# One attention block row computed by symmetry, one convolution on TensorE, and a rewritten schedule in an attention + Mamba kernel

## The chip, the cores and the metric

The kernel runs on one core of a Trainium2 chip, as one launch. The metric is the device time of one execution in microseconds (us). Time before: a median of 10092.66 us in 4 runs (10086.53 to 10095.38).

A core has five engines that run their own instruction streams side by side: PE (TensorE, matrix products; its weight loads are listed as PEld), DVE (VectorE), ACT (ScalarE), POOL (GpSimd) and SP (SyncE, which here only issues DMAs, in order). Semaphores order them.

## The reference

Eight images of 256 channels and 48 x 48 pixels go through two residual layers. Everything is float32.

```
x = x + top16_attention(group_norm(x))     # layer 0
x = x + mamba_depth_2(group_norm(x))       # layer 1

# layer 0, an image of n = 2304 tokens
feat, pos = split(tokens @ W.T + bias)     # 256 columns each
pos = pos / max(norm(pos), 1e-12)
sim = pos @ pos.T                          # 2304 x 2304
out = softmax(top16(sim)) @ feat[top16 tokens]

# layer 1, twice (d = 0, 1): 512 inner channels, 16 states
xi, z = split(layer_norm(x) @ in_w.T)
xc = silu(cb + sum_{k<4} xi[t - 3 + k] * cw[:, k])
dt_r, Bm, Cm = split(xc @ xp_w.T)          # 16 columns each
dt = softplus(dt_r @ dtp_w.T + dtp_b);  A = -exp(A_log)
h[t] = h[t-1] * exp(dt[t] A) + dt[t] Bm[t] xc[t]       # per channel and state
y = (sum_states(h * Cm) + xc * D) * silu(z)
x = y @ out_w.T
```

## The kernel before

**Layer 0** (the generator `layer0`). An image's 2304 tokens are 6 chunks of T = 384 for the statistics and projections (`project`, `features`, `norms`, `inverse_norm`, `scale`) and 18 blocks of 128 rows for the attention. `inverse_norm` starts a reciprocal root on ScalarE (L161) and finishes it with five small instructions of a Newton step on GpSimd (L168 to L172). For a block `t`, `similar` (L391) multiplies the block's positions with all 2304 positions, in five pieces of up to 512 columns and two halves of the 256 channels; `keep_similar` (L400) copies them from PSUM. `top` and `others` (L407 to L414) find the 16 largest on VectorE with two MAX8 and two MATCH_REPLACE8 over 2304 columns. What was replaced marks the chosen ones: ScalarE builds `rest` (L429), TensorE transposes similarities and subtracts a large number where nothing was chosen (`turn`, L437 and L438, tile `pt`), ScalarE exponentiates (`weights`, L446), TensorE multiplies with the features (`weigh`, L457), and the result is turned back and added to x (L464 to L487). The table `within` gives each of these pieces a place, in steps of a block that are 16 apart.

**Layer 1.** The work is cut into 96 units: 8 images x 6 chunks of 384 tokens x 2 depths. A unit has 16 steps, each for 32 inner channels; a step's tile holds 128 partitions (4 groups of states x 32 channels) and 4 states x 385 columns in its free direction. Each step is scanned in two halves. So a unit has 32 *hooks*, the whole program 3072, and the loop at the end of the file writes the order out by hand, hook by hook (manual schedule; the order in the program is the order on each engine). At hook m:

1. `carry` for the half scanned before: if its product was VectorE's, ScalarE copies the last state (`h_st`, L847) and then two zeros (L848) into the columns where the next scan restarts;
2. `decay` for the next half: two ACTIVATE exp of 384 columns into one of two PSUM banks (L815);
3. in the first half of a step: GpSimd makes the input `bx` of the step after next (`make_bx`, L791, from a ring of 8 tiles), multiplies the states of the step before with C where that is its job (`pool_part`, L860), and ScalarE or GpSimd writes the starting states (`take_up`, L805 or L803); in the second half ScalarE copies the last states that GpSimd's part leaves (`carry_pool`, L870);
4. the rows of the table `between` that fall on this hook;
5. `run_scan` (L830): a scan over 770 columns on VectorE; the restart between two sequences is a zero in the decay's first column. Where the letter in `SHARE` is "V", VectorE also multiplies with C (L832); where it is "G", `pool_part` does;
6. the rows of the table `behind`;
7. one piece of the next image's layer 0 (two until its blocks are in step with the hooks).

`SHARE` has a string of 16 letters for units 1 to 9 of an image (12 G), one for units 0, 10 and 11 (8 G) and one for the last image (8 G). The tables place a unit's own steps from 42 hooks before its first scan to 40 behind: layer norm (`mean` to `normal`), `load_in`/`in_proj` (L591), the convolution (`tap`, one ACTIVATE with the last weight, L683; `taps`, three SCALAR_TENSOR_TENSOR per 128 channels on VectorE, L691), `silu_x` (two table loads around four ACTIVATEs, L697 to L700), `x_proj`, `split` (L714, dbl<-px), `step_size`, `softplus`, `times_x` (L741), the loads of `dtr` and `dtxr` for each step (`load_rep`, rings of 3) and of B and C (`load_bc`), then `sum_states` (tile `y`: one matmul with the diagonal of D, L875, and 16 with `sel`, L878, which read the `bx` tiles of four steps), `gate`, `out_proj` and `leave`.

The first image's layer 0 has nothing to lie beside; it runs alone ahead of all this and is ordered by the framework. The projections of the next image's layer 0 all fall into unit 0 of an image, its 18 blocks into the units after. The last image has no layer 0 beside it. Between the two parts, diagonal matrices of D are made (L532), stored to HBM and loaded back one by one as `dmat`.

Of the kernel before, what the change touches and what calls it, by code (L numbers as in the profile page):

```python
# [8 lines left out]
F32 = mybir.dt.float32  # L9
BF16 = mybir.dt.bfloat16  # L10
AF = mybir.ActivationFunctionType
# [7 lines left out]
TINY = 1e-24  # L19
FAR = 64.0  # L20
# [3 lines left out]
def tile_conv_preact(  # L24
# [46 lines left out]
    SHARE = ("GGVGGGVVGGGGGGVG", "GGGVGVVGVVVGVGVG", "VGVGVGVVGGVVGGVG")  # L71
    JR = 1
# [80 lines left out]
    nc.vector.tensor_scalar(A_sb, A_sb, -1.0, None, ALU.mult)  # L153
# [74 lines left out]
    def layer0(b, left, pool, ps0, alone):  # L228
# [50 lines left out]
        def inverse_norm(c):  # L279
            rn[c] = small.tile([P, TB], F32, tag="rn", name=f"rn_{b}_{c}")  # L280
            rsqrt_start(rn[c], n2[c], tiny[:, 1:2])
            rsqrt_end(nc.gpsimd, rn[c], n2[c], TINY, f"rn_{b}_{c}")

# [11 lines left out]
        def chunk(c, xn):  # L295
# [57 lines left out]
            step(lambda: features(0), feature(0))  # L353
            yield
            if c > 0:
                scale(c - 1)
                yield
            for j in range(1, TB):
                step(lambda: features(j), feature(j))
                yield  # L360
            step(norms, norm)
# [9 lines left out]
        leave_psum()  # L371
        yield
        inverse_norm(NCH - 1)
# [11 lines left out]

        def similar(t, i):

            c0, w = widths[i]
            pm = blocks[t]["psim", i] = mm0(w, f"psim_{b}_{t}_{i}")
            for k in range(CB):  # L390
                nc.tensor.matmul(  # L391
                    pm, pos[:, k, t * P : (t + 1) * P], pos[:, k, c0 : c0 + w],
                    start=(k == 0), stop=(k == CB - 1),
                )
# [83 lines left out]
        def finish(t):  # L478
# [14 lines left out]
            (21, weights, 3), (4, top, 3), (14, turn, 0), (15, weights, 0), (6, others, 3),  # L493
            (-5, similar, 4), (-8, keep_similar, 0), (-5, keep_similar, 2), (24, turn_back), (18, weigh, 1),
            (17, weigh, 0), (1, top, 1), (-9, similar, 0), (-8, similar, 1), (-7, similar, 2),
            (22, average), (-6, similar, 3), (-7, keep_similar, 1), (-3, keep_similar, 3), (0, top, 0),
            (-3, keep_similar, 4), (15, turn, 1), (10, others, 4), (5, others, 0), (3, top, 2),
            (6, add_top), (11, invert), (5, others, 2), (17, turn, 2), (20, turn, 3),
            (15, weights, 1), (18, turn, 4), (18, weights, 2), (21, weigh, 3), (7, others, 1),
            (19, weigh, 2), (20, weights, 4), (21, weigh, 4), (24, finish),  # L500
        ]
        begin = min(part for part, *_ in within)
# [12 lines left out]

    lefts = [{} for _ in range(B)]
    with tc.tile_pool(name="first", bufs=1) as pool0, tc.tile_pool(
        name="first_ps", bufs=1, space=PSUM
    ) as ps0:
        for _ in layer0(0, lefts[0], pool0, ps0, True):  # L520
            pass

    diag = hbm.tile([P, DEPTH, DC + 1, DB, P], F32, tag="diag", name="diag", bufs=1)
    with tc.tile_pool(name="setup", bufs=2) as setup:
        for d in range(DEPTH):
            for t in range(DC, DC + 1):
                dg = setup.tile([P, DB, P], F32, tag="dg", name=f"dg_{d}_{t}")
                for k in range(DB):  # L530
                    f = cw[:, d, k, t : t + 1] if t < DC else dpar[:, d, k : k + 1]
                    nc.vector.tensor_scalar(dg[:, k], ident, f, None, ALU.mult)  # L532
                nc.sync.dma_start(diag[:, d, t], dg)
# [6 lines left out]

    banks = [ps.tile([P, 1024], F32, tag=f"da{i}", name=f"da_{i}", bufs=1) for i in range(2)]
    for bank in banks:
        nc.vector.memset(bank, 0.0)

    zeros = const.tile([P, HQ], F32, tag="zeros", name="zeros")
    nc.gpsimd.memset(zeros, 0.0)
# [12 lines left out]
    def load_rep(unit, what, ik):  # L559

        k, i0 = divmod(ik * JR, J)
        t = keep.tile([P, JR, T], F32, tag=f"{what}r", name=f"{what}r_{unit['u']}_{ik}", bufs=3)
        src = unit[f"{what}_d"][k].rearrange("(i g) t -> g i t", g=G)
        for j in range(J):
            nc.sync.dma_start(t[j * G : (j + 1) * G], src[:, i0 : i0 + JR, :])  # L565
        unit[f"{what}r"][ik] = t
# [29 lines left out]
    def load_v(unit):  # L596
        b, c = unit["b"], unit["c"]
        src = unit["left"]["x1"] if unit["d"] == 0 else unit["left"]["v1"][c]
        v = keep.tile([P, CB, T], F32, tag="v", name=f"v_{unit['u']}", bufs=1)
        if unit["d"] == 0:  # L600
            src = src[:, c * T : (c + 1) * T]
        nc.sync.dma_start(v, src.rearrange("(k p) t -> p k t", p=P))
        unit["v"] = v
# [75 lines left out]

    def tap(unit, e):  # L680
        d = unit["d"]
        o = keep.tile([P, T], F32, tag="xc", name=f"xc_{unit['u']}_{e}", bufs=7)
        nc.scalar.activation(  # L683
            o, unit["pe"][e][:, H:], AF.Identity,
            bias=cbias[:, d, e : e + 1], scale=cw[:, d, e, H : H + 1],
        )
        unit["xc"][e] = o

    def taps(unit, e):
        for k in range(H):  # L690
            nc.vector.scalar_tensor_tensor(  # L691
                unit["xc"][e], unit["pe"][e][:, k : k + T], cw[:, unit["d"], e, k : k + 1],
                unit["xc"][e], ALU.mult, ALU.add,
            )
# [77 lines left out]
    ]  # L772
    NSTEP = len(units) * STEPS
# [10 lines left out]
    def make_bx(n):  # L784


        if n >= NSTEP:
            return
        unit, i, k = at(n)
        bx = keep.tile([P, Q, 1 + T], F32, tag="bx", name=f"bx_{n}", bufs=8)  # L790
        nc.gpsimd.tensor_tensor(  # L791
            bx[:, :, 1:], unit["BC"][0],
            unit["dtxr"][i // JR][:, i % JR : i % JR + 1, :].to_broadcast([P, Q, T]), ALU.mult,
        )
        unit["bx"][i] = bx
# [11 lines left out]
    def decay(m):  # L807
# [6 lines left out]
        for s in range(HQ):  # L814
            nc.scalar.activation(  # L815
                da[:, s * (1 + T) + 1 : (s + 1) * (1 + T)], unit["dtr"][i // JR][:, i % JR, :],
# [20 lines left out]
    def carry(m):  # L837


# [4 lines left out]
        if not on_pool(unit, i, p):  # L844
# [3 lines left out]
            nc.scalar.copy(h[:, :, 0], zeros)  # L848
# [52 lines left out]
    def leave(unit, cb):  # L901
# [17 lines left out]
        (-35, center), (7, in_proj, 5), (24, sum_states, 2), (-33, variance), (-21, in_proj, 0),  # L919
        (-15, taps, 1), (38, out_proj, 0), (-15, taps, 2), (-14, taps, 3), (-34, square),  # L920
        (39, leave, 0), (23, load_rep, "dt", 14), (5, load_rep, "dt", 5), (-4, load_bc, 1), (38, out_proj, 1),
        (17, load_d, 2), (-17, tap, 1), (18, load_rep, "dtx", 13), (-8, times_x, 1), (19, gate, 1),
        (-22, normal), (1, load_rep, "dt", 3), (0, load_rep, "dtx", 4), (15, load_rep, "dt", 10), (6, load_rep, "dtx", 7),
        (10, load_rep, "dtx", 9), (12, load_rep, "dtx", 10), (20, load_rep, "dtx", 14), (11, gate, 0), (-29, spread_root),
        (-19, load_in, 5), (33, load_out), (-22, load_in, 0), (21, load_rep, "dt", 13), (-20, tap, 0),
        (-10, step_size, 1), (9, copy_z, 2), (-18, in_proj, 2), (2, load_rep, "dtx", 5), (10, sum_states, 0),
        (13, load_rep, "dt", 9), (29, gate, 2), (9, silu_z), (7, load_rep, "dt", 6), (19, load_rep, "dt", 12),
        (-6, load_rep, "dtx", 1), (-14, load_in, 7), (-30, root), (9, load_rep, "dt", 7), (4, load_d, 1),
        (-24, load_in, 3), (17, load_rep, "dt", 11), (14, load_rep, "dtx", 11), (-13, x_proj), (-17, load_in, 6),
        (-3, load_d, 0), (4, load_rep, "dtx", 6), (-4, load_rep, "dtx", 2), (-42, load_v),  # L930
    ]
    behind = [
        (-12, split), (-3, load_rep, "dt", 1), (3, in_proj, 4), (-10, step_size, 0), (-5, load_rep, "dt", 0),
        (-8, load_rep, "dtx", 0), (-15, tap, 3), (-1, load_rep, "dt", 2), (-28, scale), (16, load_rep, "dtx", 12),
        (11, load_rep, "dt", 8), (8, in_proj, 6), (17, sum_states, 1), (-14, silu_x), (25, load_rep, "dt", 15),
        (-37, affine), (1, times_x, 2), (7, copy_z, 0), (8, load_rep, "dtx", 8), (-17, tap, 2),
        (-10, softplus), (-16, in_proj, 3), (3, load_rep, "dt", 4), (-29, load_in, 2), (6, in_proj, 7),
        (35, gate, 3), (-2, load_rep, "dtx", 3), (8, copy_z, 1), (40, leave, 1), (-3, times_x, 3),
        (22, load_rep, "dtx", 15), (-16, load_in, 4), (29, load_d, 3), (-37, mean), (-19, taps, 0),
        (-19, in_proj, 1), (-10, load_bc, 0), (33, sum_states, 3), (-30, root_end), (-9, times_x, 0),  # L940
        (-22, load_in, 1),
# [90 lines left out]
```

## Time and profile before

| | us |
|---|---|
| median of 4 runs | 10092.66 |
| profiled execution | 10094.78 |
| its span | 10093.1 |
| image 0's layer 0: projections / blocks | 0 to 78 / 78 to 444 |
| unit 0 of image 0 | 501 to 645 |
| unit 0 / units 1 to 9 / units 10 and 11 of image 6 | 7794 to 7933 / to 8822.7 / to 9009 |
| the last image | 9009 to 10080 |

The mean granted clock of TensorE was 0.882 over the span. The span is the time from the first to the last instruction in the trace. "Busy" counts the time in which an engine executes; a group is all instructions of one line, operation and shape; behind the bar stand its busy time and the mean time of one in ns, and behind the second bar the time that the engine stood idle just before such instructions, with what ended most of it. `X <- Y` in a view of waits means that X waited and Y let it go.

### The profile page before, as it was taken

Reading aid. Unit: us, or ns where it says so; the run is one execution under the profiler, and the core shown is the slowest. Engines: PE = TensorE matmul, PEld = TensorE weight load, DVE = VectorE, ACT = ScalarE, POOL = GpSimd, SP = SyncE. Lnnn points to the kernel's source line nnn. Section 1 sums busy time; section 2 is a strip of 40 time slices with the busy share of each in tenths; the row PEclk is TensorE's granted clock in tenths of the full one; section 3 lists DMA queues with packets and bytes.
Section 4 is the critical chain, followed back from the end, with each engine's and each line's share of the span. In section 5 each row is a group of like instructions: output and inputs, shape, how many; then the busy total and the mean of one; then the engine's idle time right before and its main releaser. Section 6 shows DMA issues by size and latency. Waiting matters only on the chain. (4 is left out here: it accounts for less than half of the span.)

```text
span 10093.1 us, 134837 instructions
## 1 busy us (share of the span) xinstructions
PE 8015.8 (79%) x36736; PEld 4390.8 (44%) x36736; DVE 8971.1 (89%) x7992; ACT 7488.2 (74%) x16998; POOL 8943.9 (89%) x3928
## 2 busy tenths in 40 slices
PE   8878886888868888688877888778886888865655
PEld 6544443444534444344443444344443444422222
DVE  4479998899979999799997999989998899988898
ACT  4477786778767777678776777777876778777776
POOL 0079998899989999799997999989998899999998
PEclk9989997899978999799988999889997999977777
DMA  1144444444444444444444444444444444444444
GB/s 31 35 126 122 137 129 143 118 134 125 138 131 130 124 137 129 133 125 137 124 139 126 129 129 135 131 131 127 133 129 145 119 129 128 137 133 133 141 137 121
DMA packets 1243512, 1271.44 MB, mean 126 GB/s; under 512 B 266592, under 2 KB 1215840, under 8 KB 1242752
## 3 DMA queue, kind: packets, MB, share of 16 engines
q1 hardware_dynamic: 1230496, 1262.45, 43.6%
q8 instruction: 293, 4.80, 0.2%
q14 instruction: 467, 3.83, 0.1%
q10 hardware_dynamic: 12256, 0.36, 0.1%
HBM read 1048.94 MB, written 212.86 MB: 125 GB/s over the span
## 5 line engine op out<-in xcount | busy, mean ns | idle before, releaser
L791 POOL TENSOR_TENSOR bx<-BC,dtxr 128x1536 f32<-128x1536 f32 x1536 | 5303.3, 3456 | 87.0 <-PE y L878 42.1
L815 ACT ACTIVATE da<-dtr,A_sb 128x384 f32<-128x384 f32 x6144 | 3586.0, 584 | 814.3 <-DVE bx L830 619.6
L830 DVE TENSOR_TENSOR_SCAN bx<-da,bx 128x770 f32<-128x770 f32 x2040 | 3525.9, 1748 | 191.9 <-ACT da L815 143.3
L860 POOL TENSOR_TENSOR bx<-bx,BC 128x1536 f32<-128x1536 f32 (+1 forms) x1320 | 3307.5, 2506 | 256.6 <-DVE bx L830 239.7
L830 DVE TENSOR_TENSOR_SCAN da<-da,bx 128x770 f32<-128x770 f32 x1032 | 1811.0, 1755 | 247.2 <-ACT da L815 158.2
L591 PE MATMUL pe<-vn,inw 128*128 128x384 f32 (+1 forms) x3072 | 1244.0, 539 | 412.5 <-DVE xr L913 93.2
L391 PE MATMUL psim<-pos 128*128 128x512 f32 (+1 forms) x2880 | 1380.7, 612 | 205.2 <-ACT sim L400 91.7
L457 PE MATMUL po<-feat,aT 128*128 128x256 f32 x5184 | 1360.1, 411 | 20.5 <-ACT aT L446 14.3
L878 PE MATMUL y<-bx,sel 128*32 128x384 f32 x12288 | 1228.7, 536 | 40.2 <-POOL bx L860 30.3
L457 PEld LDWEIGHTS po<-feat,aT 128*128 128x128 f32 x5184 | 1028.3, 205 | 366.6 <-issue 112.7
L832 DVE TENSOR_TENSOR bx<-da,BC 128x768 f32<-128x768 f32 x1032 | 989.3, 959 | 35.5
L591 PEld LDWEIGHTS pe<-vn,inw 128*128 128x128 f32 x3072 | 584.7, 205 | 928.6 <-issue 206.9
L391 PEld LDWEIGHTS psim<-pos 128*128 128x128 f32 x2880 | 553.8, 206 | 840.3 <-issue 466.2
L878 PEld LDWEIGHTS y<-bx,sel 128*32 128x32 f32 x12288 | 397.8, 119 | 860.4 <-issue 736.0
L691 DVE SCALAR_TENSOR_TENSOR xc<-pe,cw,xc 128x384 f32<-128x384 f32 x1152 | 696.5, 612 | 38.4 <-ACT xc L683 11.4
L721 PE MATMUL pd<-dbl,dtp_sb 16*128 16x384 f32 x768 | 416.4, 656 | 342.6 <-ACT dt L730 182.4
L437 PE MATMUL pt<-ident,sim 128*128 128x128 f32 x2592 | 535.8, 289 | 41.9 <-ACT vo L909 18.0
L847 ACT COPY h_st<-da 128x2 f32<-128x2 f32 x832 | 131.6, 158 | 588.5 <-DVE bx L832 581.4
L446 ACT ACTIVATE aT<-pt 128x512 f32<-128x512 f32 (+1 forms) x720 | 387.7, 548 | 233.4 <-PE pt L438 228.8
L896 PE MATMUL pw<-z,ow 128*128 128x384 f32 x1536 | 527.4, 496 | 20.4 <-DVE v L655 7.4
L875 PE MATMUL y<-xc,dmat 128*128 128x384 f32 x768 | 392.7, 598 | 151.4 <-DVE xc L691 125.4
L429 ACT ACTIVATE rest<-left,three 128x512 bf16<-128x512 f32 (+1 forms) x720 | 467.0, 670 | 60.0 <-DVE left L414 60.0
(148 smaller groups left out, 10068.0 us busy)
## 6 DMA issues: line engine op xcount, KB each, us to landing
dtxr<-dtx_d SPq DMA_DIRECT2D x6144, 48.0 KB, 1.8
dtr<-dt_d SPq DMA_DIRECT2D x6144, 48.0 KB, 1.8
BC<-bc_d SPq DMA_DIRECT2D x768, 192.0 KB, 3.7
inw<-in_in_wT_dram SPq DMA_DIRECT2D x768, 128.0 KB, 2.3
dtx_d<-dtx SPq DMA_DIRECT2D x384, 192.0 KB, 2.0
dt_d<-dt SPq DMA_DIRECT2D x384, 192.0 KB, 2.1
ow<-in_out_wT_dram SPq DMA_DIRECT2D x96, 512.0 KB, 4.0
dmat<-diag SPq DMA_DIRECT2D x384, 64.0 KB, 2.1
```

The lines of the kernel that those rows point to most:

```text
L391: nc.tensor.matmul(pm, pos[:, k, t * P : (t + 1) * P], pos[:, k, c0 : c0 + w], start=(k == 0), stop=(k == CB - 1),)
L437: nc.tensor.transpose(pt[:, q], row["sim"][:, r], ident)
L457: nc.tensor.matmul(row["po"], aT[:, m % PT, :], feat[:, m, :], start=(m == 0), stop=(m == NB - 1))
L591: nc.tensor.matmul(pe, w[:, k], unit["vn"][:, k, lo:], start=(k == 0), stop=(k == CB - 1))
L691: nc.vector.scalar_tensor_tensor(unit["xc"][e], unit["pe"][e][:, k : k + T], cw[:, unit["d"], e, k : k + 1], unit["xc"][e], ALU.mult, ALU.add,
L791: nc.gpsimd.tensor_tensor(bx[:, :, 1:], unit["BC"][0], unit["dtxr"][i // JR][:, i % JR : i % JR + 1, :].to_broadcast([P, Q, T]), ALU.mult,)
L815: nc.scalar.activation(da[:, s * (1 + T) + 1 : (s + 1) * (1 + T)], unit["dtr"][i // JR][:, i % JR, :], AF.Exp, scale=A_sb[:, unit["d"], i, ...
L830: nc.vector.tensor_tensor_scan(h, da, g, 0.0, ALU.mult, ALU.add)
L832: nc.vector.tensor_tensor(bx[:, :, 0:T], da.rearrange("p (q t) -> p q t", q=HQ)[:, :, 1:], unit["BC"][1][:, qs], ALU.mult,)
L860: nc.gpsimd.tensor_tensor(g[:, :, 0:T], g[:, :, 1:], unit["BC"][1][:, qs], ALU.mult)
L878: nc.tensor.matmul(y[j * G : (j + 1) * G, :], sel, unit["bx"][k * J + j][:, q, 0:T], start=False, stop=True, skip_group_check=True,)
L896: nc.tensor.matmul(pw, unit["ow"][:, k, cb * P : (cb + 1) * P], unit["z"][k], start=(k == 0), stop=(k == DB - 1),)
```

## The change

1. **Symmetric similarities, in the attention that runs alone.** Each block row of `sim` is stored to HBM from its diagonal on (`store_similar`), and for a later block the sub-blocks left of its diagonal are loaded back (`load_similar`, rows of 512 bytes) and transposed on TensorE. 153 of the 324 sub-blocks of 128 x 128 are made in this way.
2. **Diagonals.** `make_diagonals` makes those of the four convolution weights beside those of D, in both depths, as piece 40 of image 0's layer 0.
3. **TensorE convolution in the last image.** `tap` copies the projected channels to SBUF, `taps` multiplies four shifted windows of them with diagonal matrices on TensorE, and the new `conv_out` adds the bias on ScalarE. The diagonals of both depths are loaded once (2 MB), with the last image's first `load_v`, into tiles that the attention has left.
4. **Restart zeros by the decays.** The `dtr` tile has one more column, set to 1e30 once, so the decay's exp writes the zero itself (385 columns); `carry` copies no zeros, the banks need no memset.
5. **Newton steps.** `inverse_norm` is split: its second half, on GpSimd, comes a piece later, after the first `features` of the next chunk; `scale` a piece after that.
6. **SHARE and the tables** are written anew: 12 G in units 1 to 9 and 8 in the last image as before, at other hooks; 9 instead of 8 in units 0, 10 and 11. Among the rows of `between` and `behind`, `sum_states` 0 moves behind the scan of hook 10 and `sum_states` 1 from behind hook 17 to behind hook 18; many loads and steps move by a few hooks. `within` is also new.

```diff
-    SHARE = ("GGVGGGVVGGGGGGVG", "GGGVGVVGVVVGVGVG", "VGVGVGVVGGVVGGVG")
+    SHARE = ("GGVGGGVVGGGVGGGG", "GGGVGVVGGGVVGVVG", "GVVVGGGVVVGGGVGV")
...
-    nc.vector.tensor_scalar(A_sb, A_sb, -1.0, None, ALU.mult)
+    nc.vector.tensor_scalar(A_sb, A_sb, LEAST, -1.0, ALU.max, ALU.mult)
...
+        def inverse_norm_end(c):
             rsqrt_end(nc.gpsimd, rn[c], n2[c], TINY, f"rn_{b}_{c}")
...
             if c > 0:
                 inverse_norm(c - 1)
-            step(lambda: features(0), feature(0))
-            yield
-            if c > 0:
-                scale(c - 1)
-                yield
-            for j in range(1, TB):
+            for j in range(TB):
                 step(lambda: features(j), feature(j))
                 yield
+                if c > 0 and j == 0:
+                    inverse_norm_end(c - 1)
+                if c > 0 and j == 1:
+                    scale(c - 1)
+                    yield
...
+        def load_similar(t, i):
+            m0, m1 = i * PT, min((i + 1) * PT, t if alone else 0)
+            if m0 < m1:
...
+                nc.sync.dma_start(old[:, 0 : m1 - m0, :], kept[:, m0:m1, t * P : (t + 1) * P])
+                blocks[t]["old", i] = old
+
+        def store_similar(t):
+            if alone and t + 1 < NB:
+                nc.sync.dma_start(kept[:, t, (t + 1) * P :], blocks[t]["sim"][:, (t + 1) * P :])
...
-            for k in range(CB):
-                nc.tensor.matmul(
-                    pm, pos[:, k, t * P : (t + 1) * P], pos[:, k, c0 : c0 + w],
...
+            for m in range(i * PT, min((i + 1) * PT, t if alone else 0)):
+                nc.tensor.transpose(pm[:, m % PT * P : (m % PT + 1) * P], old[:, m % PT, :], ident)
+            lo = max(c0, t * P if alone else 0)
+            if lo < c0 + w:
+                for k in range(CB):
+                    nc.tensor.matmul(
+                        pm[:, lo - c0 :], pos[:, k, t * P : (t + 1) * P], pos[:, k, lo : c0 + w],
...
+    steps = [keep.tile([P, 1 + T], F32, tag=f"dtr{i}", name=f"dtr_{i}", bufs=1) for i in range(3)]
+    for t in steps:
+        nc.vector.memset(t[:, 0:1], NEVER)
...
+            for e in range(DEPTH):
+                nc.sync.dma_start(late["diag"][:, e], diag[:, e, 0:DC])
...
     def tap(unit, e):
         d = unit["d"]
+        if late and unit["b"] + 1 == B:
+            nc.scalar.copy(late["xi"][:, e], unit["pe"][e])
+            return
...
     def taps(unit, e):
+        if late and unit["b"] + 1 == B:
+            cv = unit["cv"][e] = mm(T, f"cv_{unit['u']}_{e}")
+            for k in range(DC):
+                nc.tensor.matmul(
+                    cv, late["diag"][:, unit["d"], k, e], late["xi"][:, e, k : k + T],
...
+    def conv_out(unit, e):
+        if e in unit["cv"]:
...
+            nc.scalar.activation(
+                o, unit["cv"][e], AF.Identity, bias=cbias[:, unit["d"], e : e + 1]
...
-                da[:, s * (1 + T) + 1 : (s + 1) * (1 + T)], unit["dtr"][i // JR][:, i % JR, :],
+                da[:, s * (1 + T) : (s + 1) * (1 + T)], unit["dtr"][i],
...
-            nc.scalar.copy(h[:, :, 0], zeros)
...
-        (9, copy_z, 2), (-18, in_proj, 2), (2, load_rep, "dtx", 5), (10, sum_states, 0),
-        (8, in_proj, 6), (17, sum_states, 1), (-14, silu_x),
+        (18, sum_states, 1), (-19, in_proj, 1), (-18, conv_out, 0), (-14, conv_out, 2), (-14, conv_out, 3),
+        (-14, silu_x), (-39, affine), (5, times_x, 2), (-10, softplus), (-5, load_rep, "dt", 0),
+        (6, in_proj, 7), (10, sum_states, 0), (-10, times_x, 0), (-17, tap, 1), (19, load_rep, "dt", 12),
```

## The prediction

> **What bounds the kernel now.** The page gives busy shares and the dearest groups first. The profiled execution took 10094.8 us, its span 10093.1 us; the median of the runs is 2.1 us lower. The sum below starts from 10094.8 and the 2.1 us come off at its end.
>
> ```profile
> PE 8015.8 (79%) x36736; PEld 4390.8 (44%) x36736; DVE 8971.1 (89%) x7992; ACT 7488.2 (74%) x16998; POOL 8943.9 (89%) x3928
> L791 POOL TENSOR_TENSOR bx<-BC,dtxr 128x1536 f32<-128x1536 f32 x1536 | 5303.3, 3456 | 87.0 <-PE y L878 42.1
> L860 POOL TENSOR_TENSOR bx<-bx,BC 128x1536 f32<-128x1536 f32 (+1 forms) x1320 | 3307.5, 2506 | 256.6 <-DVE bx L830 239.7
> ```
>
> VectorE and GpSimd tie at 89%, but averages hide stages, so I cut the span with the windows view (start:end and length; then PE, PEld, DVE, ACT, POOL busy; granted clock; DMA share; GB/s): the attention that runs alone, unit 0 of image 6, its units 2 to 9, and the last image.
>
> ```profile
> 78.00:444.00 366.00, 354.93 (x1694) 245.19 (x1692) 208.45 (x200) 160.30 (x324) 0.00 (x0) 0.99 0.04 13
> 7794.00:7933.00 139.00, 105.99 (x467) 63.17 (x467) 93.18 (x91) 93.08 (x217) 89.76 (x89) 0.83 0.44 130
> 8029.70:8822.70 793.00, 689.92 (x3273) 386.04 (x3273) 758.68 (x671) 628.68 (x1414) 771.55 (x290) 0.93 0.46 130
> 9009.00:10080.00 1071.00, 635.27 (x2607) 269.83 (x2611) 961.95 (x823) 761.36 (x1797) 997.64 (x411) 0.76 0.47 134
> ```
>
> Each stage has another limit. Alone, TensorE is busy 97%. Unit 0 (seven times) fills no engine. Units 1 to 9 (63 of the 96) are full on GpSimd (97%) and nearly on VectorE (96%). In the last image GpSimd has 93%, VectorE 90%, TensorE 59%.
>
> **1. Symmetric similarities, 366 us alone.** The rows of that window, and the block period from the timeline (start, duration, operation, idle before):
>
> ```profile
> L391 PE MATMUL psim<-pos 128*128 128x512 f32 (+1 forms) x360 | 149.9, 558 | 0.0
> L437 PE MATMUL pt<-ident,sim 128*128 128x128 f32 x324 | 64.0, 281 | 0.0
> ```
> ```profile
> 198.88 2.56 DVE L407 MAX8 top<-sim 128x8 f32<-128x2304 f32 x1 [5.42 <-ACT sim L400]
> ...
> 206.80 2.54 DVE L414 MATCH_REPLACE8 left<-top,left 128x2304 f32<-128x2304 f32 x1
> ...
> 218.63 2.56 DVE L407 MAX8 top<-sim 128x8 f32<-128x2304 f32 x1 [5.42 <-ACT sim L400]
> ```
>
> 149.9 us / 324 sub-blocks of 128 columns = 0.46 us each. A transpose costs at most 64.0/324 = 0.20 us (the rows overlap; four transposes with their four minus products run in 0.68 us, so I take 0.11). 153 of 324 sub-blocks (0+1+...+17) change: 0.26 to 0.35 us each, about −50 us if TensorE alone set the pace. It doesn't: a block takes 19.75 us, of which the selection on VectorE holds 10.4; the next selection starts 9.4 us later, after ScalarE's rest, the attention product, and 6 us of similarities with their copies. With those gone ScalarE's own copies still need about 6 us, so a block stays above about 16.2 us. Only what is cut after the attention product counts, at most some ten sub-blocks a block: 0.33 × (1+2+...+10+3×10) = 0.33 × 85 = **−28 us**, bounds −50 and −15. The store of each finished row block and the load of the old ones (about 1.1 MB a block together) have some 13 us, and DMA stands at 4% there.
>
> **2. Diagonals earlier.** Their eight products (1.53 us), two memsets (0.91 each) and two stores leave the gap between 447 and 452 us; forty products of about 0.2 us go to the first 40 us, where VectorE is 15% busy. **−3 us**; if the x loads queued behind their ten stores on SP were late, +5.
>
> **3. TensorE convolution, last image.** Rows of the last window:
>
> ```profile
> L791 POOL TENSOR_TENSOR bx<-BC,dtxr 128x1536 f32<-128x1536 f32 x190 | 653.4, 3446 | 9.3 <-PE y L878 7.0 <-issue 2.3
> L860 POOL TENSOR_TENSOR bx<-bx,BC 128x768 f32<-128x768 f32 x144 | 314.2, 2182 | 47.5 <-DVE bx L830 46.9
> L691 DVE SCALAR_TENSOR_TENSOR xc<-pe,cw,xc 128x384 f32<-128x384 f32 x132 | 79.9, 612 | 3.1
> L848 ACT COPY da<-zeros 128x2 f32<-128x2 f32 x192 | 31.3, 163 | 40.6 <-DVE bx L832 35.5
> ```
>
> Twelve taps × 0.612 = 7.3 us leave VectorE in each of 12 units. TensorE gets 16 matmuls 384 wide, 0.9 us each by the projection rows of this window (two records, 163.2 us / 184): +14 us on 53 of 90, free as a sum. ScalarE gets four copies of 0.47 (the row dbl<-px) and four outputs of 0.58 (the decay's 0.585) for four taps of 0.66: +1.6 us. GpSimd loses nothing, and its idle time in the whole window is 73 us, 47 of it for scans. So the gain cannot pass 73; 12 × 7.3 = 88 is out of reach. I take half of the scan wait, **−25 us**, bounds −65 and +20. The loss end: conv_out 2 and 3 wait at hook −14 for eight matmuls (7 us, 12 at a low clock) with silu_x and the next decays behind them on ScalarE, and VectorE's scans wait for those. What silu_x itself holds the timeline shows:
>
> ```profile
> 9516.29 1.28 ACT L697 ACT_TABLE_LOAD   x1
> 9517.58 1.76 ACT L699 ACTIVATE xc<-xc 128x384 f32<-128x384 f32 x4
> 9519.36 1.28 ACT L700 ACT_TABLE_LOAD   x1
> ```
>
> 4.3 us, behind 9.6 us of waiting and copying at worst; the two decay banks cover about two hooks (90 us / 32 = 2.8 each), so +20 = 1.7 us in each unit. The Trainium skill ("ScalarE: Activation LUTs", "What ACT_TABLE_LOAD costs") gives 1.28 us and then a drain of 1.38 for each switch; by it the burst would be 7 us and the loss end 2.8 us a unit larger (estimate: +33). The trace agrees on the load, but its next ACTIVATE starts 0.01 us after it, so I leave the drain out. The 2 MB of late diagonals are queued once on SP ahead of the scan's loads: 7 us at 0.47 share for 136 GB/s, hidden by loads issued four hooks ahead, else +5.
>
> **4. Zeros by the decays.** 1032 copies × 163 ns leave ScalarE; in a hook whose product is VectorE's, product, carry copy, zeros and decay follow each other, so the decay comes about 0.19 us sooner. ScalarE is no limit; the saving counts only where a scan waits for it. Priced with 6. Decays read 385 columns, 1 ns more, and dtr rows land 4 bytes off: they land in 1.8 us now, and ScalarE waits 13.6 us for dtr in the whole run. [...] I keep 0.
>
> **5. Newton steps a piece later, unit 0.** Rows of GpSimd in image 5's unit 0 (last part: idle before):
>
> ```profile
> L168 POOL TENSOR_SCALAR nv_rn<-n 128x3 f32<-128x3 f32 x6 | 1.2, 196 | 21.8 <-ACT h_st L847 16.2 <-ACT n L346 5.5
> L169 POOL TENSOR_TENSOR nt_rn<-rn 128x3 f32<-128x3 f32 x6 | 1.2, 193 | 10.4 <-ACT rn L161 10.4
> ```
>
> 32 us a unit stand before these steps, with make_bx and the sums queued behind. But ScalarE and TensorE are 76% and 85% busy once x has landed (22 us of stall at the start stay), and of six chunks only one changes its place against a make_bx. I take an eighth, 4 us × 7 = **−28**, bounds −100 and +15 (the chunk's own scale comes later).
>
> **6. SHARE and the tables.** One letter more for GpSimd in units 0, 10, 11: two hooks × 1.6 = +3.2 us there against −1.9 on VectorE, in units where GpSimd is at 93% and VectorE at 88%. Half a microsecond gained in 14 units, **−7**; bounds −30, and +45 where GpSimd is full (14 × 3.2). In units 1 to 9 the letters move within the same count, sum_states 0 and 1 (17 matmuls each) go later, and loads on SP move by up to four hooks; GpSimd waits 12.8 us and ScalarE 55 us for such loads in the whole run, so a tighter load has little to lose now and is in the +60. GpSimd's floor is its idle time, 20.2 us an image × 7 = 141. VectorE waits for ScalarE about 1.5 us a unit: 0.4 × 63 = **−25**, bounds −110 and +60.
>
> Sum: −28 −3 −25 −28 −7 −25 = −116: 10094.8 − 116 − 2 = 9977 us.
>
> **Rivals.** *Only isolated stages gain* (1 and 2, with 10 to 30 us elsewhere): GpSimd's queue hides the rest, as its 97% suggests; 10030 to 10060. *Large*: unit 0 loses half of its 32 us (15 × 7 = 105) and units 1 to 9 come near the floor; ScalarE's idle time speaks for it; 9830 to 9920. *Convolution for nothing*: conv_out's wait replaces the taps; 25 less gained, about 10000, inside the forecast's range. *Slower*: make_bx reuses a ring of eight, so it waits for the y sum that reads the old tile. Sums 0 and 1 move behind the scan, the second also by a hook; its margin in the last image is 0.1 us (the 7.0 us in nine waits above). GpSimd full, each microsecond is paid: 1.5 us × 84 units (seven images of twelve) = +126, less about 100 of gains: 10115. It decides from about 1.2 us a unit. Against it: 42.1 us of such waits in the whole run now, half a microsecond a unit.
>
> **How the numbers follow.** Forecast (9930 to 10030) 0.45; isolated only 0.18; large 0.15; ring 0.12; nothing moves, gains and losses even (10072 to 10113, 0.2%, about what a measurement can tell from none) 0.10. Faster 0.78, same 0.10, slower 0.12. The range 9860 to 10095 leaves out a third of "large" (0.05), a little of "same" (0.03) and the slower rival (0.12).
>
> **What would show it.** Block period 19.75 → 17 or more late in the alone attention, VectorE's wait for sim shorter; taps gone and VectorE near 73 us in a last-image unit, GpSimd still near 84; no row of zeros; unit 0 near 135 us, its two GpSimd rows down; units 1 to 9 at 96 to 99. Wrong if make_bx waits for y for over 100 us in all, if ScalarE waits at conv_out for over 5 us a unit, or if DMA becomes the releaser of the psim transposes.

## The result and the profile after

The changed kernel takes 10103.71 us (median of 42 runs, 10092.11 to 10117.77), the kernel before 10091.53 us in the 60 runs beside it: a ratio of 1.0013, interval 1.0008 to 1.0017. The forecast was 1.1% faster. The page of the changed kernel (engines' busy time, then the rows that answer to make_bx and pool_part):

```profile
PE 8028.5 (79%) x37145; PEld 4471.4 (44%) x37145; DVE 8840.9 (88%) x7839; ACT 7331.6 (73%) x15986; POOL 9008.7 (89%) x3927
L853 POOL TENSOR_TENSOR bx<-BC,dtxr 128x1536 f32<-128x1536 f32 x1536 | 5295.2, 3452 | 155.0 <-PE y L938 113.6
L920 POOL TENSOR_TENSOR bx<-bx,BC 128x1536 f32<-128x1536 f32 (+1 forms) x1320 | 3366.7, 2551 | 226.0 <-DVE bx L892 108.1
```

VectorE has 130 us less to do, ScalarE 157, and nothing came of it. The windows view over the stages that the prediction showed (the attention alone, unit 0 of image 6, its units 2 to 9, the last image):

```profile
78.00:409.00 331.00, 306.35 (x1712) 235.98 (x1711) 206.56 (x194) 156.70 (x323) 0.00 (x0) 0.99 0.23 74
7824.40:7971.00 146.60, 110.44 (x464) 66.01 (x465) 91.41 (x89) 90.60 (x200) 97.64 (x90) 0.81 0.42 123
8068.00:8868.70 800.70, 683.04 (x3279) 392.34 (x3279) 759.17 (x671) 617.69 (x1350) 771.53 (x290) 0.93 0.45 129
9054.70:10090.00 1035.30, 723.43 (x2954) 314.75 (x2954) 877.14 (x689) 747.60 (x1649) 1001.22 (x413) 0.82 0.48 139
```

The lengths are 331.0 for 366.0, 146.6 for 139.0, 800.7 for 793.0 and 1035.3 for 1071.0 us: two stages gained, two lost. GpSimd did the same work in units 2 to 9 (771.5 us in both) and took longer over it. The experiments are read by such a table, made for each trace from the start of each unit's first scan (mean us a unit; "start" is that of the first unit, "last" the twelve units of the last image together):

| kernel | ratio to before, interval | start | unit 0 | 1 to 9 | 10, 11 | last |
|---|---|---|---|---|---|---|
| before | 1 | 501.1 | 141.3 | 98.63 | 93.2 | 1071.5 |
| after | 1.0013, 1.0008 to 1.0017 | 466.2 | 144.8 | 99.75 | 92.2 | 1035.3 |
| e1_sum1 | 1.0072, 1.0060 to 1.0085 | 466.3 | 145.5 | 99.82 | 92.4 | 1093.6 |
| e2_share1 | 1.0015, 1.0006 to 1.0023 | 467.4 | 144.3 | 100.08 | 91.7 | 1033.9 |
| e4_old_tables | 1.0056, 1.0042 to 1.0070 | 465.6 | 146.7 | 99.22 | 91.9 | 1103.3 |
| e5_newton | 1.0042, 1.0030 to 1.0055 | 498.0 | 146.9 | 98.60 | 93.2 | 1074.7 |
| e6_zeros | 0.9959, 0.9946 to 0.9971 | 496.2 | 140.2 | 98.37 | 92.0 | 1061.6 |
| e7_within | 1.0074, 1.0060 to 1.0088 | 506.3 | 140.6 | 99.67 | 93.3 | 1070.9 |
| e8_hybrid | 0.9934, 0.9921 to 0.9946 | 463.1 | 147.5 | 98.22 | 92.0 | 1035.3 |
| e9_old_within | 0.9932, 0.9920 to 0.9945 | 465.3 | 144.9 | 98.63 | 91.8 | 1035.6 |
| e10_weights4 | 1.0011, 1.0002 to 1.0020 | 463.7 | 143.0 | 99.79 | 92.2 | 1035.6 |
| e11_hybrid_no_newton | 0.9893, 0.9879 to 0.9906 | 462.8 | 139.8 | 98.43 | 91.9 | 1035.4 |
| e12_after_two | 0.9925, 0.9913 to 0.9938 | 465.9 | 143.5 | 98.45 | 92.0 | 1038.2 |
| e13_top | 0.9940, 0.9927 to 0.9954 | 463.3 | 145.0 | 98.70 | 91.7 | 1035.2 |
| e14_scale_late | 1.0035, 1.0022 to 1.0048 | 502.5 | 146.8 | 98.60 | 93.2 | 1071.5 |
| e15_no_late_conv | 1.0033, 1.0020 to 1.0046 | 467.1 | 144.0 | 99.87 | 92.1 | 1058.7 |
| e16_gpsimd_late | 0.9897, 0.9880 to 0.9913 | 463.0 | 140.7 | 98.38 | 92.0 | 1034.8 |

Against before, the changed kernel wins 35 us ahead of the first unit, 36 in the last image and 14 in units 10 and 11, and loses 7 x 3.5 = 24 in unit 0 and 63 x 1.12 = 71 in units 1 to 9: +10 us.

### The profile page after: what moved, and what is told of

It reads as the page before. It is cut to its first block, busy times and chain, and to the rows that moved or that the text cites. A ratio compares the mean times of both kernels' runs of the same rounds, so it can differ in the third digit from the quotient of the medians.

```text
span 10102.2 us, 134581 instructions
## 1 busy us (share of the span) xinstructions
PE 8028.5 (79%) x37145; PEld 4471.4 (44%) x37145; DVE 8840.9 (88%) x7839; ACT 7331.6 (73%) x15986; POOL 9008.7 (89%) x3927
## 4 chain that ended last, share of the span: by engine, by line
DVE 29%; PE 22%; ACT 18%; issue 9%; SPq 9%; DMA 8%; POOL 3%; ACTq 0%; POOLq 0%; DVEq 0%
DVE bx L892 9%; SPq L599 7%; ACT da L877 7%; DVE da L892 6%; PE psim L419 5%; DMA dtxr<-dtx_d 4%; PE y L938 3%; PE pe L625 2%; DVE left L438 2%; PE po L485 2%; DVE top L440 2%; DVE bx L894 2%; PE px L766 2%; DVE top L435 2%; DVE xc L744 2%
## 5 line engine op out<-in xcount | busy, mean ns | idle before, releaser
L853 POOL TENSOR_TENSOR bx<-BC,dtxr 128x1536 f32<-128x1536 f32 x1536 | 5295.2, 3452 | 155.0 <-PE y L938 113.6
L877 ACT ACTIVATE da<-dtr,A_sb 128x385 f32<-128x385 f32 x6144 | 3590.2, 585 | 864.0 <-DVE bx L892 493.3
L892 DVE TENSOR_TENSOR_SCAN bx<-da,bx 128x770 f32<-128x770 f32 x2082 | 3604.0, 1747 | 337.8 <-ACT da L877 275.1
L920 POOL TENSOR_TENSOR bx<-bx,BC 128x1536 f32<-128x1536 f32 (+1 forms) x1320 | 3366.7, 2551 | 226.0 <-DVE bx L892 108.1
L892 DVE TENSOR_TENSOR_SCAN da<-da,bx 128x770 f32<-128x770 f32 x990 | 1738.9, 1756 | 229.0 <-ACT da L877 91.8
L419 PE MATMUL psim<-pos 128*128 128x512 f32 (+1 forms) x2752 | 1325.8, 619 | 291.1 <-DVE z L944 90.3
L625 PE MATMUL pe<-vn,inw 128*128 128x384 f32 (+1 forms) x3072 | 1206.8, 525 | 369.6 <-ACT da L877 129.3
L938 PE MATMUL y<-bx,sel 128*32 128x384 f32 x12288 | 1289.7, 538 | 157.2 <-POOL bx L920 150.3
L894 DVE TENSOR_TENSOR bx<-da,BC 128x768 f32<-128x768 f32 x990 | 948.5, 958 | 34.1
L744 DVE SCALAR_TENSOR_TENSOR xc<-pe,cw,xc 128x384 f32<-128x384 f32 x1008 | 609.5, 611 | 39.1 <-ACT xc L728 12.7
L428 ACT COPY sim<-psim 128x512 f32<-128x512 f32 (+1 forms) x720 | 378.8, 536 | 282.2 <-PE psim L419 274.8
L935 PE MATMUL y<-xc,dmat 128*128 128x384 f32 x768 | 380.6, 581 | 205.4 <-DMA dmat<-diag 140.2
```

The source lines that it names most:

```text
L419: nc.tensor.matmul(pm[:, lo - c0 :], pos[:, k, t * P : (t + 1) * P], pos[:, k, lo : c0 + w], start=(k == 0), stop=(k == CB - 1),)
L625: nc.tensor.matmul(pe, w[:, k], unit["vn"][:, k, lo:], start=(k == 0), stop=(k == CB - 1))
L744: nc.vector.scalar_tensor_tensor(unit["xc"][e], unit["pe"][e][:, k : k + T], cw[:, unit["d"], e, k : k + 1], unit["xc"][e], ALU.mult, ALU.add,
L853: nc.gpsimd.tensor_tensor(bx[:, :, 1:], unit["BC"][0], unit["dtxr"][i].unsqueeze(1).to_broadcast([P, Q, T]), ALU.mult,)
L877: nc.scalar.activation(da[:, s * (1 + T) : (s + 1) * (1 + T)], unit["dtr"][i], AF.Exp, scale=A_sb[:, unit["d"], i, p * HQ + s : p * HQ + s ...
L892: nc.vector.tensor_tensor_scan(h, da, g, 0.0, ALU.mult, ALU.add)
```

## The experiments

### First theory: the ring of bx tiles (e1 to e4)

GpSimd's idle time in units 1 to 9 rose from 2.2 to 3.4 us a unit, and most of the rise stood ahead of the make_bx that waits for `sum_states` 1. That was the slower rival of the prediction. Three edits of the changed kernel, e1 and e2 as diffs:

```diff
-        (18, sum_states, 1),
+        (17, sum_states, 1),
```
```diff
-    SHARE = ("GGVGGGVVGGGVGGGG", "GGGVGVVGGGVVGVVG", "GVVVGGGVVVGGGVGV")
+    SHARE = ("GGVGGGVVGGGVGGGG", "GGGVGVVGVVVGVGVG", "GVVVGGGVVVGGGVGV")
```

and, in e4, SHARE, `between` and `behind` as before, with the new rows ahead of `silu_x`:

```diff
+        (-18, conv_out, 0), (-14, conv_out, 1), (-14, conv_out, 2), (-14, conv_out, 3), (-14, silu_x),
```

> The changed kernel with sum_states 1 put back from behind hook 18 to behind hook 17. Ring theory: units 1 to 9 of images 0 to 6 lose 71 us against before, and 89 us of GpSimd's idle time there stands ahead of the make_bx of step 12, which reuses a tile that sum_states 1 reads. With the sum a hook earlier that wait falls below 20 us, units 1 to 9 return to 98.7 us or less each, the whole gets 45 to 90 us faster than the changed kernel (ratio to before 0.993 to 0.998). Letters theory: the new SHARE letters and load hooks hold GpSimd elsewhere; the wait goes but GpSimd then waits as long for the scans of its pool parts, less than 20 us gained (ratio 1.000 to 1.002).

> The changed kernel with the old SHARE letters (8 G) in units 0, 10 and 11 only. If unit 0's loss of 3.4 us against before is GpSimd's extra letter (its sums are 3 us a unit dearer there), unit 0 gets 2 to 5 us shorter, 15 to 35 us in seven images, and units 10 and 11 lose 1 to 2 us each (+14 to +28 us): the whole within 15 us of the changed kernel. If the loss in unit 0 comes from the Newton steps or from loads instead, unit 0 stays within 1 us, and the whole gets 10 to 25 us slower by units 10 and 11.

> The changed kernel with the SHARE strings and the tables between and behind as before (and the rows for conv_out added next to silu_x): parts 1 to 5 of the change without part 6. If the tables are the loss: the attention alone keeps its -35 us, the last image -10 to -36 us, units 1 to 9 at 98.3 to 98.7 us, unit 0 at 137 to 141 us; the whole 45 to 90 us faster than before (ratio 0.991 to 0.9955). If the parts themselves cost (385-column decays, dtr rows 4 bytes off, Newton steps a piece later), units 1 to 9 stay near 99.7 us and unit 0 near 145 us, and the whole is within 30 us of before.

The ring theory falls. In e1 the waits of that make_bx halved (89 to 45 us in units 1 to 9), and those units stayed at 99.8 us: GpSimd waited elsewhere (its idle time there was 217 us and is 216). The whole got slower, all of it in the last image (+58 us): `sum_states` 1 now stands ahead of the convolution's matmuls on TensorE, and ScalarE's conv_out waits for them. The waits view of the last image, of e1 and then of the changed kernel (total us, times, longest):

```profile
ACT xc L752 <- PE cv L738: 72.9, 27, 5.0
```
```profile
ACT xc L752 <- PE cv L738: 14.0, 14, 1.8
```

e4 shows the same in its last image (90.0 us of such waits, 1103.3 us). So the later place of `sum_states` 1 serves the convolution. (A longer ring should take the wait itself away, but e3, with nine tiles, has no time: its pool needs 204.4 KB per partition where 198.5 are left.) e2 tells that the ninth letter is worth nothing measurable either way. e4 also showed that old tables do not cure unit 0 and units 1 to 9: what costs there is another part.

### One part at a time on the kernel before (e5, e6, e7), and a hybrid (e8)

e5 has only part 5, e6 only part 4, e7 only the new `within` without its store and loads. e8 is the changed kernel with the old tables (`between0`, `behind0`), letters and `within` wherever an attention lies beside the scans:

```diff
+        if not alone:
+            within = [
...
+        last = unit["b"] + 1 == B
-        for table, rows in ((inner, between), (outer, behind)):
+        for table, rows in ((inner, between if last else between0), (outer, behind if last else behind0)):
```

> The kernel before with the Newton steps a piece later and nothing else. With the old tables and parts 1 to 5, unit 0 was 146.7 us against 141.3. If Newton's new place is the cause (scale comes a piece later, so positions of the chunk and all that waits for them), unit 0 gets 3 to 6 us longer, 20 to 40 us in all, units 1 to 9 unchanged. If it works as forecast, unit 0 gets 2 to 6 us shorter, -15 to -40 us. If it is neither, within 1 us a unit.

> The kernel before with the restart zeros made by the decays and nothing else. If it helps as forecast: units 1 to 9 0.1 to 0.5 us shorter each, the last image too, -10 to -50 us. If decays that no longer wait behind a zeros copy meet other work earlier (ScalarE's order against TensorE's matmuls) or the 385-column rows cost: units 1 to 9 0.3 to 0.7 us longer, +20 to +45 us.

> The kernel before with the new order of the attention's pieces (the table within, without store_similar and load_similar) and nothing else; it also orders the attention that runs alone, without symmetry. If the new order is what makes units 1 to 9 longer: +0.4 to +1.1 us each, +25 to +70 us, with ScalarE's waits for the transposes (pt) near hook 25 rising from below 50 us to some 250 us. If not: within 0.2 us a unit.

> The changed kernel with the old tables between and behind, the old letters and the old order of the attention's pieces wherever an image has an attention beside it (images 0 to 6), and the new ones in the last image and in the attention alone. If the new tables are right for the last image and wrong for the others: attention alone -35 us, last image -36 us, units 1 to 9 within 0.3 us of 98.6, unit 0 within 2 us of 141: the whole -50 to -80 us against before (ratio 0.992 to 0.995), faster than both kernels. If the zeros or the Newton steps cost by themselves, units 1 to 9 or unit 0 stay long, and it is within 30 us of before.

The medians give **zeros -42 us, Newton steps +42, within +75**. The zeros gain in every stage, most where VectorE has many products: about 0.3 us in a unit with 4 such letters (units 1 to 9), 0.8 to 1.2 us in a unit with 8 (the others). `within` alone makes units 1 to 9 as long as in the changed kernel (99.67), and ScalarE's waits for transposes rose as expected (229 and 108 us), which made `weights` 4 look guilty.

### Which row of within (e9, e10, e13)

e9 puts back the whole old `within` beside the scans (the first two lines of e8's diff), e10 one row, e13 two:

```diff
-        (19, weights, 4),
+        (20, weights, 4),
```
```diff
-        (1, top, 0), (2, top, 1),
+        (0, top, 0), (1, top, 1),
```

> The changed kernel with the old order of the attention's pieces (within) beside the scans, the new one only where the attention runs alone. If the costs and gains of the parts add up (within +75 us on the kernel before), units 1 to 9 fall from 99.75 to 98.3 to 98.9 us, unit 0 stays near 145, and the whole is 55 to 90 us faster than the changed kernel (ratio to before 0.992 to 0.996). If the new tables were fitted to the new within, the old one fits them worse, and the gain is below 30 us.

> The changed kernel with one row of within put back: weights 4 (ScalarE's exp of the last transposes) from part 19 to 20. With within alone on the kernel before, ScalarE's waits for the transposes rose from 47 and 42 us to 229 and 108 us (near hooks 25 and 8), as its instruction now stands in front of the decays before turn 4 has been done. If that is the cost: those waits fall below 120 us together, and 40 to 80 us are gained on the changed kernel (ratio to before 0.9935 to 0.9975). If the cost lies in the other moved rows (others 3 and 4, top 0 and 1, invert): less than 15 us.

> The changed kernel with two rows of within put back: top 0 (the first MAX8) from part 1 to 0 and top 1 (the first MATCH_REPLACE8) from part 2 to 1, also in the attention alone. Cover theory: in units 1 to 9 these two lay on VectorE while ScalarE works through softplus with its two table loads (5.5 us near hook 22); a piece later only one of them does, the scan of hook 24 waits 1.3 us for its decay, the other then delays the scan of hook 25, and GpSimd's product of that step waits 2.2 us instead of 0.3. Put back: units 1 to 9 from 99.75 to 98.2 to 98.9 us, GpSimd's waits for scans near hooks 25 and 29 from 111 us to below 40, and the whole 50 to 90 us faster than the changed kernel (ratio to before 0.992 to 0.9965). If the others rows (parts 6 to 9 and 10 to 12) or similar 2 are the cost: less than 15 us.

`weights` 4 explains nothing (1.0011 for 1.0013, units 1 to 9 at 99.79). ScalarE's 212 us of waits for transposes at hook 25 of these units are gone in e10 and the time stays: they were idle time of an engine that had room. The two selection rows explain nearly all: e13 is 66 us faster than the changed kernel, units 1 to 9 at 98.70, where the whole old `within` gives 98.63. The windows of image 6's units 2 to 9, of e7 and of e13:

```profile
8090.00:8889.40 799.40, 681.85 (x3273) 385.45 (x3274) 759.12 (x672) 627.55 (x1415) 771.70 (x290) 0.94 0.45 129
8004.40:8795.80 791.40, 672.73 (x3272) 382.74 (x3271) 759.19 (x672) 617.89 (x1350) 771.84 (x290) 0.95 0.49 130
```

The time is lost at one place. From the scan of hook 22 to that of hook 25 a unit takes 12.0 us in e13 and 13.3 us in the changed kernel (mean of the 63 units 1 to 9); the rest of the unit is 0.2 us shorter in the changed kernel. GpSimd's waits near hooks 25 and 29 of these units sum to 111 us in the changed kernel and to 31 in e13. The timeline shows why. Near hook 22 ScalarE works through softplus between two table loads, from 8200.87 to 8206.36 us in the kernel before (unit 3 of image 6). VectorE there (start, duration, operation, idle before), and GpSimd's product of the step:

```profile
8201.53 2.55 DVE L407 MAX8 top<-sim 128x8 f32<-128x2304 f32 x1
...
8206.73 2.54 DVE L410 MATCH_REPLACE8 left<-top,sim 128x2304 f32<-128x2304 f32 x1
8209.19 3.40 DVE L830 TENSOR_TENSOR_SCAN bx<-da,bx 128x770 f32<-128x770 f32 x2
```
```profile
8212.74 3.17 POOL L860 TENSOR_TENSOR bx<-bx,BC 128x1536 f32<-128x1536 f32 x1 [0.34 <-DVE bx L830]
```

The MAX8 lies inside the burst and the MATCH_REPLACE8 beside the first decays after it (8206.76 to 8209.56), and then two scans run back to back. The same place in e7, on ScalarE, VectorE and GpSimd:

```profile
8265.70 1.28 ACT L736 ACT_TABLE_LOAD   x1
...
8267.38 1.20 ACT L815 ACTIVATE da<-dtr,A_sb 128x384 f32<-128x384 f32 x2
```
```profile
8264.82 2.55 DVE L407 MAX8 top<-sim 128x8 f32<-128x2304 f32 x1
8268.68 1.76 DVE L830 TENSOR_TENSOR_SCAN bx<-da,bx 128x770 f32<-128x770 f32 x1 [1.31 <-ACT da L815]
...
8270.41 2.54 DVE L410 MATCH_REPLACE8 left<-top,sim 128x2304 f32<-128x2304 f32 x1
8272.87 1.75 DVE L830 TENSOR_TENSOR_SCAN bx<-da,bx 128x770 f32<-128x770 f32 x1
```
```profile
8274.77 3.18 POOL L860 TENSOR_TENSOR bx<-bx,BC 128x1536 f32<-128x1536 f32 x1 [2.17 <-DVE bx L830]
```

Only the MAX8 lies beside the burst: the scan waits 1.31 us for its decay, the MATCH_REPLACE8 then comes between the two scans, and GpSimd, which is full in these units, waits 2.17 us for the second instead of 0.34. 1.8 us here, 1.0 to 1.1 on the mean of 63 units.

### Which half of the Newton move (e14, e16), and the last image (e15)

e14 is the kernel before with `scale` behind the second `features`; e16 is e11 (below) with GpSimd's half right ahead of a `scale` that keeps its place; e15 is the changed kernel without the load that turns its convolution on:

```diff
-            step(lambda: features(0), feature(0))
-            yield
-            if c > 0:
-                scale(c - 1)
-                yield
-            for j in range(1, TB):
+            for j in range(TB):
                 step(lambda: features(j), feature(j))
                 yield
+                if c > 0 and j == 1:
+                    scale(c - 1)
+                    yield
```
```diff
             if c > 0:
+                inverse_norm_end(c - 1)
                 scale(c - 1)
                 yield
```
```diff
-        if unit["b"] + 1 == B and not late:
+        if False:
```

> The kernel before with the Newton steps in their old place and only scale a piece later. If the loss of 41 us with the whole move comes from scale (the positions' product on VectorE waits for TensorE's spread a piece later, with scans behind it): unit 0 +3 to +6 us, the whole +20 to +45 us. If it comes from GpSimd's five instructions standing behind another make_bx: unit 0 within 1.5 us, the whole within 12 us.

> The fastest version so far (old tables, letters and within for images 0 to 6, new ones in the last image, old place of scale; 9983.6 us, ratio 0.9893) with only GpSimd's half of the Newton steps a piece later, right in front of scale, which keeps its place. If GpSimd's 50 us of idle time in unit 0 is worth anything, as the forecast had it: 2 to 6 us less in unit 0, 15 to 40 us off. If unit 0 is held by the chain from a chunk's norms to its scaled positions, the five instructions (1.5 us) now lie in that chain right before scale: 0 to 3 us more in unit 0, up to 20 us slower than the fastest version.

> The changed kernel with the last image's convolution back on VectorE and everything else as changed (tables, letters, zeros). The last image took 1071 us before, 1062 with the zeros alone, 1035 in the changed kernel. If the TensorE convolution brings the rest: 1055 to 1075 us without it, the whole 20 to 40 us slower than the changed kernel. If the new tables and letters bring it: within 8 us of the changed kernel.

`scale` alone costs 33 us of e5's 42, and unit 0 is as long as there (146.8 and 146.9 us). GpSimd's half alone wins nothing (9981.9 for 9983.6 us; the intervals of the two ratios overlap). It did not shorten GpSimd's idle time before the Newton steps either (31.4 us in a unit 0 for 32.3 in e11, mean of seven), so what that time would be worth is not shown. The timeline at hook 15 of image 6's unit 0, of the kernel before and of e14 (VectorE):

```profile
7867.20 0.95 DVE L289 TENSOR_TENSOR pos<-pos,pb 128x768 f32<-128x768 f32 x1 [0.22 <-PE pb L218]
```
```profile
7906.88 0.95 DVE L289 TENSOR_TENSOR pos<-pos,pb 128x768 f32<-128x768 f32 x1 [5.25 <-PE pb L218]
```

The Newton steps end 3.6 us before TensorE's spread (pb) begins in the one (7862.76, 7866.34) and 8.6 us before it in the other (7897.36, 7905.94): the norms were not what it waited for. It stood behind one more `features` and its copy, and VectorE's product stood in front of the next scan all that time. In the seven unit 0s this wait at hook 15 grows from 0.2 to 4.9 us on the mean; those of the same product at hooks 18 and 25 (3.9 and 4.3 us before) go, but other waits take their place, and the unit ends 5.5 us longer. Whether pb was let go by ScalarE's copy (ended 7905.79) or by GpSimd's make_bx (7905.87) the trace does not settle.

In the last image the convolution on TensorE is worth 23 of the 36 us (1058.7 without it); zeros, tables and letters bring the rest.

### The faster version (e11, e12)

e11 is e8 with the Newton steps and `scale` in their old places; e12 is e9 with the same.

> The run with the old tables, letters and within for images 0 to 6 and the new ones for the last image, now with the Newton steps in their old place. If the parts add up: unit 0 from 147.5 to 141 us or less, 35 to 50 us faster than with the Newton steps moved, 100 to 125 us faster than before (ratio 0.9875 to 0.990). If the old tables already hide the Newton steps: within 15 us of that run.

> The changed kernel with two things undone: within beside the scans and the Newton steps, so new tables and letters, zeros, symmetry and the TensorE convolution stay. If the parts add up: 100 to 130 us faster than the changed kernel, 90 to 120 us faster than before (ratio 0.988 to 0.991). If the new tables have a cost of their own in images 0 to 6 (the wait of make_bx for sum_states 1), it is 20 us or more slower than the run with the old tables and the old Newton place.

e11 takes 9983.61 us, ratio 0.9893 (0.9879 to 0.9906): faster than both kernels by 108 and 120 us. e12 is 30 us slower, 7 x 3.7 = 26 of them in unit 0: the new tables and letters cost there. Which row does it was not tried. With them the Newton move loses little (e9 to e12: 13 us), with the old ones 37 (e8 to e11), so the parts do not simply add. On the way from e11 to the changed kernel the losses are 30 us for tables and letters (e12), 13 for the Newton move (e9) and 77 for `within`: 120. The windows of e11 (unit 0 of image 6, units 2 to 9, the last image):

```profile
7716.50:7856.90 140.40, 107.34 (x466) 64.13 (x467) 93.21 (x92) 90.78 (x202) 90.13 (x89) 0.83 0.44 129
7952.60:8742.50 789.90, 687.98 (x3273) 386.00 (x3272) 758.59 (x671) 619.24 (x1350) 772.44 (x290) 0.93 0.46 131
8928.90:9964.00 1035.10, 721.37 (x2952) 316.86 (x2944) 877.43 (x690) 747.68 (x1649) 999.03 (x412) 0.82 0.49 139
```

## Why the prediction was wrong, step by step

The measured time lies in the prediction's box "nothing moves, gains and losses even" (10072 to 10113, chance 0.10). Much moved, though: stages with gains of 85 us and stages with losses of 95 nearly cancel. That the sum is near zero is luck.

- **Steps 1 and 2, -28 and -3:** 35 us ahead of the first unit. Right, and the mechanism of step 1 too. The block period (MAX8 to MAX8) of the changed kernel is 19.3 us in early blocks, falls by about a third of a microsecond from one block to the next and is 15.8 us in the last three (19.75 before); what it falls below 19.3 sums to 28 us. VectorE's wait for `sim` goes down with it, from 5.42 to 2.03 us. Only the floor of 16.2 that ScalarE's copies were taken to set was a little too high. Two other parts work there too: e6, which drops the memsets, starts 5 us sooner without symmetry (496.2), and e7, with the new order of the pieces, 5 us later (506.3). The diagonals were not run by themselves.

```profile
304.96 2.56 DVE L435 MAX8 top<-sim 128x8 f32<-128x2304 f32 x1 [2.85 <-ACT sim L428]
...
321.43 2.56 DVE L435 MAX8 top<-sim 128x8 f32<-128x2304 f32 x1 [2.54 <-ACT sim L428]
...
369.17 2.56 DVE L435 MAX8 top<-sim 128x8 f32<-128x2304 f32 x1 [1.83 <-ACT sim L428]
...
384.93 2.56 DVE L435 MAX8 top<-sim 128x8 f32<-128x2304 f32 x1 [2.03 <-ACT sim L428]
```

- **Step 3, -25:** right (23 by e15), and the mechanism too. GpSimd's wait for scans in the last image, of which half was to go, was 46.9 us before, 27.8 in e15 and 4.1 in the changed kernel, so the convolution took 24 of it. Its waits for y (7.0 before, 14.4 after) did not rise by the convolution: e15 has 20.5. The loss end of +20 is real as well: in e1 ScalarE waits 72.9 us for the convolution's matmuls, 6.1 us a unit, over the 5 that the prediction set as a sign, and the last image takes 1093.6 us, 22 more than before the change. That the place of `sum_states` 1 decides between the two was not seen.
- **Step 4, priced with 6:** the zeros were worth 42 us by themselves, more than the 25 for both. The decays of 385 columns take 586 ns for 585, as foreseen. Decays waited 13.6 us for dtr before and 20.0 in e6, and dtr landed in 1.8 us in both; 6 us between two profiled executions can neither show nor exclude a cost of rows that land 4 bytes off.
- **Step 5, -28: failed in sign**, +42 alone and +13 beside the new tables. The step took an eighth of GpSimd's idle time before the Newton steps for time that could be won, and put the later `scale` at +15 at most. e14 shows that the later `scale` costs 33 us by itself. e16 shows that moving GpSimd's half alone neither wins time nor shortens that idle time.
- **Step 6, -7 and -25: failed.** Units 10 and 11 gave -14, but not by the extra letter: the zeros alone bring them to 92.0 us (e6), and without the letter they take 91.7 (e2). Units 1 to 9 gave +71 where -25 was forecast and +60 was the bound. The step that failed is a term that was never made: the new `within` was listed as part of the change, and no term prices its moved rows, so they stood at nothing without a reason. e7 puts them at +75. Two of them moved by one piece; on VectorE they had lain beside ScalarE's softplus burst, and putting these two back wins 66 us (e13). In unit 0 the new tables and letters cost 26 us more (e11 to e12), which the step had no term for either; the cause of that stays open.
- **The slower rival** named the wrong place. (Its sum comes to 10119, not 10115.) Waits of make_bx for y rose to 113.6 us, just over the 100 us that the prediction had set as the sign for it; e1 and e9 show the sign to be false: in e9 these waits still sum to 108 us in units 1 to 9, where the changed kernel has 78, and the units are back at 98.63.

## What to carry to other kernels

An engine that waits in front of an instruction does not say that this instruction is late: when GpSimd is full, its idle time can move to the next place when one wait is taken away (e1), and idle time of an engine with room can be free (e10). Ask of every moved row what it lay beside: here two searches of 2.55 us that moved by one piece, away from another engine's table loads, cost 1.05 us a unit on the mean of 63. Where a change joins several parts, run each alone on the old kernel first; here losses of 120 us hid gains of 108.

## What the hardware showed that was not expected

The granted clock of TensorE in the last image rose from 0.76 to 0.82, and a projection matmul there fell from 593 to 523 ns. It took the convolution and the new tables together: the new tables with the convolution on VectorE give 0.77 and 567 ns (e15), the convolution with the old tables 0.78 and 589 ns (e4). With the tables alike, from e15 to the changed kernel, 176 more matmuls cost TensorE 69 us of busy time (723 for 654), less than their own 119. The matmuls of the changed kernel, and the windows of the last image of e15 and of e4:

```profile
L738 PE MATMUL cv<-late_xi,late_diag 128*128 128x384 f32 x352 | 119.0, 490 | 8.6 <-ACT late_xi L725 8.5
```
```profile
9060.00:10114.00 1054.00, 654.40 (x2599) 267.29 (x2592) 949.87 (x819) 731.96 (x1599) 995.87 (x411) 0.77 0.51 136
9029.00:10132.00 1103.00, 755.90 (x2960) 345.10 (x2964) 882.30 (x691) 749.05 (x1649) 996.94 (x411) 0.78 0.46 130
```

The Trainium skill ("TensorE: Matmul & The Clock Gate", "What's actually happening") says that the throttled state is the default and that activity releases it. The rise from 0.77 to 0.82 agrees with that. But the share of busy time alone does not tell the clock: e4 is busy 69% of its last image and has 0.78, the changed kernel 70% and 0.82, e1 68% (743 of 1094 us) and 0.82. What in the order of the work makes the difference no run here shows.
